# Four edits in one kernel: constants, the search, token numbers, and the order of work beside the last experts

## The chip, the cores and the metric

The kernel runs on one core of one Trainium2 chip. The metric is the time of one execution on the device in microseconds (us). The core has a matrix engine (PE, TensorE), a vector engine (DVE), a scalar engine (ACT), a general engine (POOL, GpSimd) and an engine that here only issues transfers (SP). Each runs its own instructions in order and waits on the others by semaphores. Transfers (DMAs) are issued into queues by SP, ACT or POOL and are carried out by 16 DMA engines.

## What is computed

The reference takes x of 8 x 512 tokens with 256 features. It adds to x the normalised output of an attention block with its MLP, and then the normalised output of a mixture of 8 experts. Cut to what matters here (`_layernorm` is a normalisation over the features):

```python
def experts(x, gate_w, ln_w, ln_b, fc1s, b1s, fc2s, b2s):
    xf = x.reshape(-1, d)                         # 4096 tokens, d = 256
    scores = softmax(xf @ gate_w.T)               # 4096 x 8
    vals, idx = top_k(scores.T, k)                # each expert keeps its best k = 512 tokens
    y = layernorm(xf[flat_idx].reshape(k, n, d)) * ln_w + ln_b
    h = gelu(einsum('knd,nfd->knf', y, fc1s) + b1s)          # 1024 hidden features
    out = (einsum('knf,ndf->knd', h, fc2s) + b2s) * kept_w[..., None]
    return xf.at[flat_idx].add(out.reshape(k * n, d))        # added back to the tokens' rows

x = x + _layernorm(attention_and_mlp(_layernorm(x)))
x = x + _layernorm(experts(_layernorm(x)))
```

A token may be kept by several experts or by none, so a token's row is final only when every expert that kept it has added its part.

## The kernel before

**Sizes.** P = 128 partitions, T = 4096 tokens in 8 blocks of 512 (4 tiles of 128), E = 8 experts, CAP = 512 tokens per expert in NJ = 4 tiles, NF = 8 slices of 128 hidden features, NC = 32 tiles of tokens in all.

**First stage.** It loads the weights, then for each block normalises x, computes performer attention, the MLP and the gate's logits. Constants are made first, among them the ones of the later search (lines 86 to 122): `mod_i`, `same` (a bf16 matrix that adds up the 16 partitions that hold one expert's scores), `before`, `ones_w`, `pcol`, `ccol`, `lane`, `jcol`. `pj` (line 217) is a tile that POOL sets to zero, eight small loads on ACT's queue fill, and DVE scales (line 223). Weights w1 and w2 (lines 230, 231) and the blocks of x (line 204) are loaded by SP, in this order. In this stage a planner orders the instructions of blocks that overlap.

**Search.** The 4096 x 8 scores are turned so that each partition holds 256 scores of one expert. `largest` (lines 778 to 802) finds the threshold of each expert bit by bit, 15 steps for the high bits and 15 for the low ones. A step counts on DVE the keys at or above the candidate `u` (`junk`, with the sum written to `cnt`), adds the counts over the expert's partitions on PE (`ptot`, with `same`), and gets the next candidate on DVE (`un` from `ptot` and `eb`). `low_bits` puts a few DVE instructions between.

**Token numbers.** From the threshold each kept token gets a slot from 0 to 511 (`hi` is the tile, `lo` the row in it). `mark(e)` builds on DVE a one-hot tensor `hot` (128 x 128 x 32, bf16) of `lo`, and `num` (the token's number in two parts, for the slot's tile). `number(e)` multiplies them on PE, 32 matmuls into `pi`, and DVE makes from it `idx`, the token number of every slot. `gather(e)` fetches with `idx` the token rows, by indirect DMAs that POOL issues.

**Experts.** For each expert: `hidden(e, f)` for f = 0 to 7 (two matmuls, then ACT's gelu into `hTe`), `weighted(e, j)` for j = 0 to 3 (eight matmuls, then ACT and DVE make `o`), and `add_rows(e, j)`, which adds `o` by an indirect DMA with addition to the table `accs`, for e < 4 also to the table `acc` (each scatter is preceded by a tiny memset `apart`). Beside it run `gather`, `normalised` (DVE), `keep_scores`, and `turn` (PE transposes, ACT copies) for the next expert, and the load of the expert's weights w1e, w2e after the next.

**Second half.** Here the experts' work and the last normalisation overlap. The tokens' rows in `acc` hold the sum over experts 0 to 3. For a block b of 512 tokens, `load_z` loads it on SP (buffers: 4, shared with `hot`), `S` takes mean and variance on DVE and the root on POOL (`ln_stats`, lines 129 to 138: `st`, `mv`, `rs`), `A` normalises on ACT (four activations with `nb`, a DVE instruction, lines 153 to 163), `X` adds the residual on DVE and stores the block to `out` on SP. The tokens that experts 4 to 7 keep get their final rows afterwards: `gather_sum(e)` fetches rows of `accs` into `zg` (POOL), `sum_rows` adds the expert's own `o`, `SR`, `AR`, `XR` do for them what `S`, `A`, `X` do for blocks, and `put_rows` writes them to `out` by four scatters (POOL). In the last expert this is done per tile (`finish_row`).

**Order.** From line 714 on the order is written by hand: each engine takes its instructions in the order of the program's text. `at(e, f, fn)` puts `fn` behind hidden(e, f) for f = 0 to 7, behind weighted(e, f - 8) for f = 8 to 11. Functions of one place run in the order of their registration: the loads of weights at (e, 0) and the gathers first, the list `plan` last. In `plan` a, b, c, d are experts 4, 5, 6, 7. `behind` makes a reader of a table, or the first scatter of another expert's group into it, wait for the landing of the last group of scatters.

Of the kernel before, what the change touches and what calls it, by code (L numbers as in the profile page):

```python
# [9 lines left out]
F32 = mybir.dt.float32  # L10
BF = mybir.dt.bfloat16
# [14 lines left out]
def performer_moe_kernel(  # L26
# [60 lines left out]
    mod_i = sp.tile([P, P], I32, name="mod_i")  # L87
    nc.gpsimd.iota(mod_i, pattern=[[-1, P]], base=P, channel_multiplier=1)
    nc.vector.tensor_scalar(mod_i, mod_i, E - 1, None, ALU.bitwise_and)

    same = sp.tile([P, P], BF, name="same")
    nc.vector.tensor_scalar(same, mod_i, 0.0, None, ALU.is_equal)
    before = sp.tile([P, P], BF, name="before")
    nc.gpsimd.affine_select(
        out=before, in_=same, compare_op=ALU.is_gt, fill=0.0,
        base=0, pattern=[[1, P]], channel_multiplier=-1,
    )
    ones_w = sp.tile([P, 2 * P], BF, name="ones_w")
    nc.gpsimd.memset(ones_w, 1.0)
    one_c = sp.tile([P, 1], F32, name="one_c")  # L100
    nc.gpsimd.memset(one_c, 1.0)
    pcol = sp.tile([P, 1], F32, name="pcol")
    nc.gpsimd.iota(
        pcol, pattern=[[0, 1]], base=0, channel_multiplier=1,
        allow_small_or_imprecise_dtypes=True,
    )

    ccol = sp.tile([P, NC, NJ], BF, name="ccol")
    nc.gpsimd.iota(
        ccol, pattern=[[1, 2], [2, NC // 2], [0, NJ]], base=0, channel_multiplier=0,  # L110
        allow_small_or_imprecise_dtypes=True,
    )
    lane = sp.tile([P, P, NC], BF, name="lane")
    nc.gpsimd.iota(
        lane, pattern=[[1, P], [0, NC]], base=0, channel_multiplier=0,
        allow_small_or_imprecise_dtypes=True,
    )
    jcol = sp.tile([P, NC, NJ], BF, name="jcol")
    nc.gpsimd.iota(
        jcol, pattern=[[0, NC], [1, NJ]], base=0, channel_multiplier=0,  # L120
        allow_small_or_imprecise_dtypes=True,
    )
# [70 lines left out]
    with ExitStack() as attn:  # L193
# [523 lines left out]
        for b in range(NB + 1):  # L717
            steps = [attention(b)] if b < NB else []
            steps += [mlp(b - 1)] if 0 <= b - 1 < NB else []
            steps += [gate(b - 2)] if 0 <= b - 2 < NB else []  # L720
            while steps:
                steps = [s for s in steps if next(s, s) is not s]
        with tc.manual_schedule():
            last(NB - 1)
# [53 lines left out]
    def largest(keys, tag, beside):  # L778


        u = one_c
        for i in range(15):

            scale = 2.0 ** -(14 if i == 0 else 15 - i)
            junk = rp.tile([P, W], BF, tag="junk", name=f"junk_{tag}{i}")
            cnt = small.tile([P, 1], BF, tag="cnt", name=f"cnt_{tag}{i}")
            with nc.allow_low_precision(reason="whole numbers up to 256"):
                nc.vector.scalar_tensor_tensor(
                    junk, keys, scale, u.to_broadcast([P, W]), ALU.mult, ALU.is_ge,
                    accum_out=cnt,  # L790
                )
            pt = ps_sm.tile([P, 1], F32, tag="sm", name=f"ptot_{tag}{i}")
            nc.tensor.matmul(pt, same, cnt, start=True, stop=True)
            eb = small.tile([P, 1], F32, tag="eb", name=f"eb_{tag}{i}")
            nc.vector.tensor_scalar(
                eb, u, 1.0 if i == 0 else 2.0, -0.5, ALU.mult, ALU.add
            )
            next(beside, None)
            un = small.tile([P, 1], F32, tag="un", name=f"un_{tag}{i}")
            nc.vector.scalar_tensor_tensor(un, pt, CAP - 0.5, eb, ALU.is_ge, ALU.add)  # L800
            u = un
        return u
# [3 lines left out]
    nc.vector.tensor_scalar(hs, uh, -0.5, 32768.0, ALU.add, ALU.mult)  # L806
# [5 lines left out]
    nc.vector.tensor_scalar(tl_, ul, -0.5, None, ALU.add)  # L812
# [45 lines left out]

    def mark(e, lo_e):


        num = ep.tile([P, NC, 2, NJ], BF, tag="num", name=f"num_{e}")
        nc.vector.tensor_tensor(
            num[:, :, 0, :], hi[:, e, :].unsqueeze(2).to_broadcast([P, NC, NJ]), jcol,
            ALU.is_equal,
        )
        nc.vector.tensor_tensor(num[:, :, 1, :], num[:, :, 0, :], ccol, ALU.mult)
        nc.vector.tensor_scalar(num[:, :, 0, :], num[:, :, 0, :], pcol, None, ALU.mult)
# [9 lines left out]
    def number(e):  # L878

        hot, num = hots.pop(e)  # L880
        pi = ps_sm.tile([P, 2, NJ], F32, tag="sm", name=f"pi_{e}")
        for q in range(NC):
            nc.tensor.matmul(
                pi.rearrange("p a j -> p (a j)"), hot[:, :, q],
                num[:, q, :, :].rearrange("p a j -> p (a j)"),
                start=(q == 0), stop=(q == NC - 1),
            )
        tl = small.tile([P, NJ], F32, tag="tl", name=f"tl_{e}")
        nc.vector.tensor_scalar(tl, pi[:, 1, :], float(P), None, ALU.mult)
        idx = rp.tile([P, NJ], I32, name=f"idx_{e}")  # L890
        nc.vector.tensor_tensor(idx, pi[:, 0, :], tl, ALU.add)  # L891
        idxs[e] = idx
# [146 lines left out]
    def sum_rows(e, j):  # L1039
        zj = zgs[e][:, j, 0:D]  # L1040
        nc.vector.tensor_tensor(zj, zj, rows_o[e][:, j, :], ALU.add)

    def SR(e):
        lns["r", e] = ln_stats(zgs[e], NJ, f"r{e}")
# [47 lines left out]
    for e in range(2, E):  # L1092
# [7 lines left out]
        else:  # L1100
            for j in range(NJ):
                at(e - 1, j, gather, e, range(j, j + 1))
            at(e - 1, 6, normalised, e)
            at(e - 1, 6, keep_scores, e)
# [4 lines left out]
    for e in range(L0, E):  # L1109
        for j in range(NJ):  # L1110
            at(e, (3 if e == E - 1 else 4) + j, gather_sum, e, range(j, j + 1))
            at(e, 8 + j, sum_rows, e, j)

    for b in range(3):
        at(L0, 1, load_z, b)
    a, b, c, d = range(L0, E)
    plan = [
        (a, 4, load_z, 3), (a, 6, S, 0), (a, 8, A, 0), (a, 8, S, 1), (a, 9, X, 0),
        (a, 9, load_z, 4), (a, 10, A, 1), (a, 10, S, 2), (a, 11, X, 1), (a, 11, load_z, 5),
        (a, 11, A, 2),  # L1120
        (b, 0, X, 2), (b, 0, load_z, 6), (b, 0, S, 3), (b, 2, A, 3, range(0, 2)),
        (b, 3, A, 3, range(2, 4)), (b, 4, X, 3), (b, 4, load_z, 7), (b, 4, S, 4),
        (b, 6, A, 4, range(0, 2)), (b, 7, A, 4, range(2, 4)), (b, 8, X, 4), (b, 8, S, 5),
        (b, 10, A, 5), (b, 10, SR, a), (b, 11, X, 5), (b, 11, AR, a),
        (c, 0, XR, a), (c, 0, S, 6), (c, 2, A, 6, range(0, 2)), (c, 3, A, 6, range(2, 4)),
        (c, 4, X, 6), (c, 4, S, 7), (c, 6, A, 7, range(0, 2)), (c, 7, A, 7, range(2, 4)),
        (c, 8, X, 7), (c, 8, SR, b), (c, 10, AR, b), (c, 11, XR, b),
        (d, 0, put_rows, a), (d, 1, SR, c), (d, 3, AR, c, range(0, 2)),
        (d, 4, AR, c, range(2, 4)), (d, 5, XR, c), (d, 7, put_rows, b), (d, 9, put_rows, c),
    ]  # L1130
# [3 lines left out]
    for e in range(E):  # L1134
# [12 lines left out]
        for j in range(NJ):  # L1147
# [5 lines left out]
            if e == E - 1:  # L1153
                if j > 0:
                    finish_row(e, j - 1)
                    if j == NJ - 1:
                        put_rows(e, range(j))
# [53 lines left out]
```

## Time and profile before

| | us |
|---|---|
| median of three runs | 1137.06 (1136.58 to 1138.34) |
| the profiled execution | 1131.89 |
| its span in the profile | 1130.2 |
| search, 30 steps | 802.99 to 830.3 |
| first matmul of the first `number` | 839.28 |
| expert 4, 5, 6, 7: first matmul of hidden | 981.03, 1009.45, 1050.35, 1083.86 |
| last matmul ends | 1111.58 |
| last scatter on POOL ends | 1122.30 |

The span is from the first to the last instruction of one execution that the hardware profiler recorded; the time of that execution is 1.7 us more. Times within the profile are us from the span's start. The page's rows give a line of the kernel, the engine, the operation, the tiles (written <- read) and the shapes, then total busy time, the mean in ns, and the engine's idle time ahead of the instruction with what released it. "Granted clock" is the share of PE's full speed that the throttle allowed: 0.901 over the span.

### The profile page before, as it was taken

To read this page: it belongs to the slowest core of one execution; us is meant where nothing else is said; L and a number is where in the kernel's file an instruction comes from. 1 tells how busy PE (TensorE), PEld (TensorE's weight loads), DVE (VectorE), ACT (ScalarE), POOL (GpSimd) and SP (SyncE) were. 2 spreads that over 40 slices of the span, in tenths; PEclk is the share of its full clock that TensorE was granted. 3 is DMA by queue.
4 is the path that set the end of the run, shared out by engine and by line. 5 is a ranking of instruction groups with operands and counts; after the bars stand their busy time and mean duration, and the time that the engine had idled before them with its cause. 6 is when DMAs were issued, how large, how long until landed. Compare 5 with 4: busy or idle time off the path is not lost. (4 is left out here: it accounts for less than half of the span.)

```text
span 1130.2 us, 13031 instructions
## 1 busy us (share of the span) xinstructions
PE 973.5 (86%) x4772; PEld 710.2 (63%) x4772; DVE 601.7 (53%) x1662; ACT 332.4 (29%) x618; POOL 298.5 (26%) x400
## 2 busy tenths in 40 slices
PE   2898997997999899799799799959229999997893
PEld 1685685586577568468568657848118677664562
DVE  3725637737745765773773755564762332144533
ACT  0322412423333232241332333222004222334540
POOL 5002003101200400310310120032311665555675
PEclk9958999989999999998998989979558999998997
DMA  6000000300300300120020020020531565588841
GB/s 221 1 1 1 1 1 1 113 1 1 113 1 1 112 2 1 46 68 1 1 94 1 1 94 2 1 82 13 179 111 55 107 130 119 128 274 266 235 101 56
DMA packets 61856, 77.12 MB, mean 68 GB/s; under 512 B 8032, under 2 KB 52576, under 8 KB 61664
## 3 DMA queue, kind: packets, MB, share of 16 engines
q1 hardware_dynamic: 51056, 58.87, 15.9%
q0 software_dynamic: 9920, 16.41, 7.3%
q10 hardware_dynamic: 816, 1.00, 0.3%
q8 instruction: 38, 0.62, 0.2%
q14 instruction: 26, 0.21, 0.1%
HBM read 43.09 MB, written 33.18 MB: 67 GB/s over the span
## 5 line engine op out<-in xcount | busy, mean ns | idle before, releaser
L494 PE MATMUL ph<-xaT,w_sb 128*128 128x512 f32 (+1 forms) x288 | 132.2, 587 | 0.5 <-ACT xaT L190 0.5
L1004 PE MATMUL pwe<-w2e,hTe 128*128 128x256 f32 x512 | 117.3, 387 | 6.7 <-ACT hTe L993 6.7
L989 PE MATMUL phe<-yT,w1e 128*128 128x512 f32 (+1 forms) x288 | 117.7, 567 | 4.0 <-ACT hTe L993 4.0
L520 PE MATMUL pm<-w_sb,hT 128*128 128x256 f32 x448 | 120.7, 433 | 0.0
L326 POOL TENSOR_TENSOR xn<-xn,rows_sb 128x1024 f32<-128x1024 f32 x8 | 18.7, 2341 | 364.5 <-PE pt_x L189 364.5
L1004 PEld LDWEIGHTS pwe<-w2e,hTe 128*128 128x128 f32 x512 | 98.6, 195 | 24.0 <-ACT hTe L993 8.2
L520 PEld LDWEIGHTS pm<-w_sb,hT 128*128 128x128 f32 x448 | 97.5, 222 | 18.0 <-issue 2.3
L989 PEld LDWEIGHTS phe<-yT,w1e 128*128 128x128 f32 x288 | 57.1, 200 | 58.1 <-issue 48.6
L494 PEld LDWEIGHTS ph<-xaT,w_sb 128*128 128x128 f32 x288 | 53.9, 203 | 42.6 <-issue 34.6
L385 PEld LDWEIGHTS pc<-v_aug,kp 128*128 128x128 f32 x512 | 66.9, 210 | 7.0 <-issue 3.0
L498 ACT ACTIVATE hT<-ph,cols_sb 128x512 f32<-128x512 f32 (+1 forms) x72 | 45.8, 636 | 85.9 <-PE ph L494 85.9
L409 ACT ACTIVATE qd<-qd 128x1024 f32<-128x1024 f32 x32 | 33.8, 1056 | 123.1 <-DVE qd L404 123.1
L434 PEld LDWEIGHTS po<-ctxb,qpT 128*128 128x128 f32 x512 | 64.8, 205 | 8.2 <-ACT qpT L424 4.6
L434 PE MATMUL po<-ctxb,qpT 128*128 128x34 f32 x512 | 67.2, 289 | 1.3
L385 PE MATMUL pc<-v_aug,kp 128*128 128x34 f32 x512 | 66.8, 293 | 0.9 <-DVE kp L379 0.9
L424 ACT ACTIVATE qpT<-ptq 128x512 f32<-128x512 f32 x64 | 35.2, 595 | 101.2 <-PE ptq L419 101.2
L524 DVE TENSOR_TENSOR r<-pm,r 128x256 f32<-128x256 f32 x28 | 11.9, 425 | 95.0 <-PE pm L520 95.0
L909 POOL DMA_INDIRECT accs<-o,idx x28 | 46.1, 1646 | 59.1 <-DVE o L1008 39.4
L993 ACT ACTIVATE hTe<-phe,cols_sb 128x512 f32<-128x512 f32 (+1 forms) x72 | 45.0, 636 | 54.2 <-PE phe L989 51.9
L375 ACT ACTIVATE kp<-kp,nstab 128x256 f32<-128x256 f32 x128 | 52.7, 495 | 20.7 <-DVE nstab L353 20.7
L1008 DVE SCALAR_TENSOR_TENSOR o<-b2s_sb,gg,o 128x256 f32<-128x256 f32 x32 | 15.5, 483 | 75.2 <-ACT o L1007 73.3
L895 POOL DMA_INDIRECT y<-xg,idx x32 | 35.0, 1095 | 65.4 <-DVE idx L891 38.5
(213 smaller groups left out, 1679.4 us busy)
## 6 DMA issues: line engine op xcount, KB each, us to landing
w1e<-in_f SPq DMA_DIRECT2D x8, 1024.0 KB, 8.3
w2e<-in_f SPq DMA_DIRECT2D x8, 1024.0 KB
z<-acc SPq DMA_DIRECT2D x8, 1024.0 KB
x<-in_x_in SPq DMA_DIRECT2D x8, 512.0 KB, 6.0
accs<-x SPq DMA_DIRECT2D x8, 512.0 KB, 4.0
acc<-x SPq DMA_DIRECT2D x8, 512.0 KB, 4.5
xg<-xf SPq DMA_DIRECT2D x8, 512.0 KB
accs<-xf SPq DMA_DIRECT2D x8, 512.0 KB, 4.2
```

Of the source, the lines that this page charges most:

```text
L375: nc.scalar.activation(kp[:, :, h, :], kp[:, :, h, :], AF.Exp, bias=nstab[:, h : h + 1])
L385: nc.tensor.matmul(pc[:, hp, :, :].rearrange("p a d -> p (a d)"), kp[:, t, pair, :].rearrange("p h m -> p (h m)"), v_aug[:, t, pair, :].re ...
L424: nc.scalar.activation(qpT[:, 4 * g : 4 * g + 4, :], pt, AF.Copy, bias=RATIO * EPS_K, scale=RATIO,)
L434: nc.tensor.matmul(po[:, 2 * hp : 2 * hp + 2, :].rearrange("p a d -> p (a d)"), qpT[:, hp, :], ctxb[:, hp, :, :].rearrange("p a d -> p (a ...
L494: nc.tensor.matmul(ph, w1_sb[:, c, ts(f, P)], xaTs[b][:, c, cols], start=(c == 0), stop=(c == KD - 1),)
L498: nc.scalar.activation(hTs[b][:, f, cols], ph, AF.Relu, bias=cols_sb[:, C_B1 + f : C_B1 + f + 1])
L520: nc.tensor.matmul(pw, hT[:, f, ts(t, P)], w2_sb[:, f, :], start=(f == 0), stop=(f == NF - 1),)
L895: this = nc.gpsimd.indirect_dma_start(out=dst, out_offset=None, in_=table[:, :], in_offset=bass.IndirectOffsetOnAxis(ap=idx[:, j : j + 1], ...
L909: this = nc.gpsimd.indirect_dma_start(out=table[:, :], out_offset=bass.IndirectOffsetOnAxis(ap=idxs[e][:, j : j + 1], axis=0), in_=src, in ...
L989: nc.tensor.matmul(ph, w1e[:, c, ts(f, P)], yT[:, c, cols], start=(c == 0), stop=(c == KD - 1))
L993: nc.scalar.activation(hTs[e][:, f, cols], ph, AF.Gelu_apprx_tanh, bias=cols_sb[:, col : col + 1])
L1004: nc.tensor.matmul(pw, hT[:, f, ts(j, P)], w2e[:, f, :], start=(f == 0), stop=(f == NF - 1))
```

## The change

The four parts:

- **Constants.** The block of lines 87 to 122 moves behind the steps of block 0 in the first stage. New constants come with it: `same_far` (`same` times 2^18), `bias_c`, `top`, `bit_steps` (15 pairs, written by 30 small memsets).
- **Search.** The count is a `tensor_scalar` against `u` as a per-partition operand instead of a `scalar_tensor_tensor` against `u` broadcast. A bias matmul opens the sum on PE, the count's matmul with `same_far` ends it, so that `ptot` is a large number with the sign of the answer; `un` clamps it between the two next candidates `lh`.
- **Token numbers.** In `number` the operands change sides: a slice of `num` with 32 columns is held in PE and `hot` streams, and four matmuls write to four groups of 32 partitions of `pq`. DVE copies `pq` to `quarters`, and an fp32 matmul with `pick` adds up the four groups into `pi`. `num` lies in two fixed tiles, set to zero once.
- **Order beside experts 4 to 7.** `plan` is rewritten, `normalised` and `keep_scores` go from (e-1, 6) to (e-1, 7) for the late experts, `sum_rows` of all four tiles becomes part of `SR`, and the last expert's `put_rows` goes in pieces of 2, 1 and 1 tiles instead of 3 and 1.

```diff
@@ constants: the moved block stands behind the steps of block 0 @@
+            if b > 0:
+                continue
+            mod_i = sp.tile([P, P], I32, name="mod_i")
...
+            FAR = 2.0 ** 18
+            same_far = sp.tile([P, P], BF, name="same_far")
+            nc.vector.tensor_scalar(same_far, same, FAR, None, ALU.mult)
+            bias_c = sp.tile([P, 1], BF, name="bias_c")
+            nc.gpsimd.memset(bias_c, -float(CAP // (P // E)))
+            nc.gpsimd.memset(bias_c[0:E, :], 0.5 - float(CAP // (P // E)))
+            top = sp.tile([P, 1], F32, name="top")
+            nc.gpsimd.memset(top, 2.0 ** 14 - 0.5)
+            bit_steps = sp.tile([P, 15, 2], F32, name="bit_steps")
+            for i in range(15):
+                down, up = (-(2.0 ** (13 - i)), 2.0 ** (13 - i)) if i < 14 else (-1.0, 0.0)
+                nc.gpsimd.memset(bit_steps[:, i, 0:1], down)
+                nc.gpsimd.memset(bit_steps[:, i, 1:2], up)
...
@@ def largest(keys, tag, beside): @@
+            nc.tensor.matmul(pt, same_far, bias_c, start=True, stop=False)
             with nc.allow_low_precision(reason="whole numbers up to 256"):
-                nc.vector.scalar_tensor_tensor(
-                    junk, keys, scale, u.to_broadcast([P, W]), ALU.mult, ALU.is_ge,
-                    accum_out=cnt,
+                nc.vector.tensor_scalar(
+                    junk, keys, u, 0.0, ALU.is_ge, ALU.add, accum_out=cnt
                 )
-            pt = ps_sm.tile([P, 1], F32, tag="sm", name=f"ptot_{tag}{i}")
-            nc.tensor.matmul(pt, same, cnt, start=True, stop=True)
-            eb = small.tile([P, 1], F32, tag="eb", name=f"eb_{tag}{i}")
-            nc.vector.tensor_scalar(
-                eb, u, 1.0 if i == 0 else 2.0, -0.5, ALU.mult, ALU.add
-            )
+            nc.tensor.matmul(pt, same_far, cnt, start=False, stop=True)
+            lh = small.tile([P, 2], F32, tag="lh", name=f"lh_{tag}{i}")
+            nc.vector.tensor_tensor(lh, u.to_broadcast([P, 2]), bit_steps[:, i, :], ALU.add)
             next(beside, None)
             un = small.tile([P, 1], F32, tag="un", name=f"un_{tag}{i}")
-            nc.vector.scalar_tensor_tensor(un, pt, CAP - 0.5, eb, ALU.is_ge, ALU.add)
+            nc.vector.scalar_tensor_tensor(
+                un, pt, lh[:, 0:1], lh[:, 1:2], ALU.max, ALU.min
+            )
@@ ahead of mark @@
+    CT = P // 4
+    nums = []
+    for i in range(2):
+        nm = rp.tile([P, NC, CT], BF, name=f"num{i}")
+        nc.gpsimd.memset(nm, 0.0)
+        nums.append(nm)
+    pick_i = rp.tile([P, CT], I32, name="pick_i")
+    nc.gpsimd.iota(pick_i, pattern=[[-1, CT]], base=P, channel_multiplier=1)
+    nc.vector.tensor_scalar(pick_i, pick_i, CT - 1, None, ALU.bitwise_and)
+    pick = rp.tile([P, 2 * NJ], F32, name="pick")
+    nc.vector.tensor_scalar(pick, pick_i[:, 0 : 2 * NJ], 0.0, None, ALU.is_equal)
@@ def number(e): @@
         hot, num = hots.pop(e)
+        pq = ps_sm.tile([P, P], F32, tag="sm", name=f"pq_{e}")
+        for r in range(NC // 4):
+            for c in range(4):
+                q = 4 * r + c
+                nc.tensor.matmul(
+                    pq[c * CT : (c + 1) * CT, :], num[:, q, :], hot[:, :, q],
+                    start=(r == 0), stop=(r == NC // 4 - 1),
+                )
+        quarters = small.tile([P, P], F32, tag="quarters", name=f"quarters_{e}", bufs=2)
+        nc.vector.tensor_copy(quarters, pq)
         pi = ps_sm.tile([P, 2, NJ], F32, tag="sm", name=f"pi_{e}")
-        for q in range(NC):
-            nc.tensor.matmul(
-                pi.rearrange("p a j -> p (a j)"), hot[:, :, q],
-                num[:, q, :, :].rearrange("p a j -> p (a j)"),
-                start=(q == 0), stop=(q == NC - 1),
-            )
+        nc.tensor.matmul(
+            pi.rearrange("p a j -> p (a j)"), quarters, pick, start=True, stop=True
+        )
@@ the second half @@
-    def sum_rows(e, j):
-        zj = zgs[e][:, j, 0:D]
-        nc.vector.tensor_tensor(zj, zj, rows_o[e][:, j, :], ALU.add)
+    def sum_rows(e, js=range(NJ)):
+        zg = zgs[e][:, js[0] : js[-1] + 1, 0:D]
+        nc.vector.tensor_tensor(zg, zg, rows_o[e][:, js[0] : js[-1] + 1, :], ALU.add)
 
     def SR(e):
+        sum_rows(e)
         lns["r", e] = ln_stats(zgs[e], NJ, f"r{e}")
...
-            at(e - 1, 6, normalised, e)
-            at(e - 1, 6, keep_scores, e)
+            at(e - 1, 7, normalised, e)
+            at(e - 1, 7, keep_scores, e)
...
-            at(e, 8 + j, sum_rows, e, j)
-
-    for b in range(3):
-        at(L0, 1, load_z, b)
     a, b, c, d = range(L0, E)
     plan = [
-        (a, 4, load_z, 3), (a, 6, S, 0), (a, 8, A, 0), (a, 8, S, 1), (a, 9, X, 0),
-        (a, 9, load_z, 4), (a, 10, A, 1), (a, 10, S, 2), (a, 11, X, 1), (a, 11, load_z, 5),
-        (a, 11, A, 2),
-        (b, 0, X, 2), (b, 0, load_z, 6), (b, 0, S, 3), (b, 2, A, 3, range(0, 2)),
-        (b, 3, A, 3, range(2, 4)), (b, 4, X, 3), (b, 4, load_z, 7), (b, 4, S, 4),
-        (b, 6, A, 4, range(0, 2)), (b, 7, A, 4, range(2, 4)), (b, 8, X, 4), (b, 8, S, 5),
-        (b, 10, A, 5), (b, 10, SR, a), (b, 11, X, 5), (b, 11, AR, a),
-        (c, 0, XR, a), (c, 0, S, 6), (c, 2, A, 6, range(0, 2)), (c, 3, A, 6, range(2, 4)),
-        (c, 4, X, 6), (c, 4, S, 7), (c, 6, A, 7, range(0, 2)), (c, 7, A, 7, range(2, 4)),
-        (c, 8, X, 7), (c, 8, SR, b), (c, 10, AR, b), (c, 11, XR, b),
-        (d, 0, put_rows, a), (d, 1, SR, c), (d, 3, AR, c, range(0, 2)),
-        (d, 4, AR, c, range(2, 4)), (d, 5, XR, c), (d, 7, put_rows, b), (d, 9, put_rows, c),
+        (a, 1, load_z, 0), (a, 3, load_z, 1), (a, 5, load_z, 2), (a, 6, S, 0), (a, 8, S, 1),
+        (a, 8, load_z, 3), (a, 10, A, 0), (a, 10, S, 2), (a, 11, X, 0), (a, 11, A, 1),
+        (b, 0, S, 3), (b, 0, load_z, 4), (b, 1, X, 1), (b, 2, A, 2, range(0, 2)),
+        (b, 2, load_z, 5), (b, 3, A, 2, range(2, 4)), (b, 4, S, 4), (b, 4, X, 2),
+        (b, 5, A, 3, range(0, 2)), (b, 5, load_z, 6), (b, 6, A, 3, range(2, 4)),
+        (b, 6, S, 5), (b, 7, X, 3), (b, 8, A, 4), (b, 8, load_z, 7), (b, 8, SR, a),
+        (b, 9, X, 4), (b, 10, A, 5), (b, 10, S, 6), (b, 11, X, 5), (b, 11, AR, a),
+        (c, 0, S, 7), (c, 1, XR, a), (c, 2, A, 6, range(0, 2)), (c, 3, A, 6, range(2, 4)),
+        (c, 3, SR, b), (c, 4, X, 6), (c, 5, A, 7, range(0, 2)), (c, 6, A, 7, range(2, 4)),
+        (c, 7, X, 7), (c, 10, AR, b), (c, 11, XR, b),
+        (d, 0, SR, c), (d, 0, put_rows, a), (d, 2, AR, c, range(0, 2)),
+        (d, 3, AR, c, range(2, 4)), (d, 4, XR, c), (d, 7, put_rows, b), (d, 8, put_rows, c),
     ]
...
@@ the loop over experts, in the last expert's weighted @@
                 if j > 0:
                     finish_row(e, j - 1)
-                    if j == NJ - 1:
-                        put_rows(e, range(j))
+                if j == 2:
+                    put_rows(e, range(0, 2))
+                if j == 3:
+                    put_rows(e, range(2, 3))
+                sum_rows(e, range(j, j + 1))
                 lns["r", e, j] = ln_stats(zgs[e][:, j : j + 1, :], 1, f"r{e}_{j}")
```

## The prediction, made before the changed kernel ran

> **What bounds it now.** I read the page first: its totals, the 40 slices, then the span in windows by stage, what PE waited for, and the order of time on each engine around those waits.
>
> ```profile
> span 1130.2 us, 13031 instructions
> PE 973.5 (86%) x4772; PEld 710.2 (63%) x4772; DVE 601.7 (53%) x1662; ACT 332.4 (29%) x618; POOL 298.5 (26%) x400
> PE   2898997997999899799799799959229999997893
> PEclk9958999989999999998998989979558999998997
> DMA  6000000300300300120020020020531565588841
> ```
> A slice is 28.3 us. PE is at 9 or more in most of them: until about 800 us (attention and its MLP) and again from 840 (the experts) matmuls set the time. The two 2s (slices 29 and 30) are the search, a ladder of tiny steps between DVE and PE; the last digit is the tail without matmuls. In the second half of the experts the DMA row rises to 8.
>
> ```profile
> 985.00:1018.00 33.00, 31.48 (x112) 20.10 (x110) 13.96 (x42) 11.86 (x22) 20.00 (x23) 1.00 0.89 273
> 1018.00:1050.00 32.00, 25.88 (x87) 17.84 (x88) 15.54 (x46) 14.80 (x28) 19.30 (x21) 0.84 0.84 262
> 1050.00:1084.00 34.00, 30.94 (x108) 20.50 (x107) 16.69 (x49) 16.60 (x32) 21.76 (x26) 0.95 0.70 192
> 1084.00:1112.00 28.00, 27.57 (x97) 17.91 (x95) 10.13 (x25) 9.64 (x18) 21.41 (x33) 1.00 0.35 97
> ```
> Columns: stretch, length, busy PE, PEld, DVE, ACT, POOL, granted clock, DMA share, GB/s. Expert 4 is within the first row, 5 within the first and second, 6 in the third, 7 in the fourth: only 5 and 6 lose PE time, and with it clock (0.84).
>
> ```profile
> PE pwe L1004 <- ACT hTe L993: 6.7, 2, 3.7
> PE phe L989 <- ACT hTe L993: 4.0, 1, 4.0
> ```
> These are all of PE's waits after 980 us: three, 10.7 us, each for hTe, ACT's output. The first shows what held ACT up:
>
> ```profile
> 1014.73 1.67 POOL L136 TENSOR_SCALAR rs_z<-mv_z 128x4 f32<-128x4 f32 x1
> 1016.49 1.04 POOL L137 TENSOR_TENSOR rs_z<-rs_z,mhalf 128x4 f32<-128x4 f32 x1
> ```
> ```profile
> 1017.76 2.07 ACT L161 ACTIVATE z<-z,nb_z,rs_z 128x256 f32<-128x256 f32 x4 [3.56 <-DVE nb_z L156]
> 1019.74 1.81 ACT L993 ACTIVATE hTe<-phe,cols_sb 128x512 f32<-128x512 f32 x3
> ```
> ```profile
> 1020.46 2.08 PE L989 MATMUL phe<-yT,w1e 128*128 128x512 f32 x2 [3.98 <-ACT hTe L993]
> ```
> POOL's root for block 2 (S, 2) ended at 1017.5, ACT sat in A(2) ahead of hTe, PE idled 3.98. Undisturbed, an expert takes 28.4 us (e4: 981.03 to 1009.45; it is 8 × 1.717 hidden, 4 × 3.46 weighted, 1.04 turn). e5 took 40.9 (1009.45 to 1050.35), e6 33.5 (to 1083.86): 17.6 us over, 10.7 of it waits, the rest a slow clock after them (16 matmuls 10.05 us instead of 7.03 after the first).
>
> **The late plan.** Loads. z0 to z3 wait for the scatters into acc and for buffers, not for PE, and SP runs ahead: all four went at 990.6 to 993.1, and in the new places they go at the same time. That "spread" costs and brings nothing. SP's queue matters later:
>
> ```profile
> 1006.55 0.38 SPq L1035 DMA_DIRECT2D out<-z  x1
> 1009.48 0.36 SPq L1016 DMA_DIRECT2D z<-acc  x1
> ...
> 1019.75 0.56 SPq L738 DMA_DIRECT2D w1e<-in_f  x1
> 1020.36 0.46 SPq L740 DMA_DIRECT2D w2e<-in_f  x1
> ```
> z4 needs z0's buffer, so it follows the landing of out0 (2.9 us). Now X(0) is issued at (a,11), some 5.5 us later (1012), and w1e, w2e of expert 6, registered at (b,0) ahead of load_z 4, go before z4: 2 MB at 262 to 273 GB/s are 7.8 us, z4's 1 MB 3.9, so z4 lands near 1012.5 + 7.8 + 3.9 = 1024.2.
>
> Roots. S(0) and S(1) move ahead, A(0) behind the last two outputs of expert 4, A(2) to (b,2): the 3.98 wait at 1016 should go, with about 3 us of clock. But DVE's new order is S(4), X(2), nb of block 3: S(4) waits for z4, and behind it stands what A(3) and so hTe need. z4 1024.2 + S(4) 2.3 (4 × 0.401, 4 × 0.182) + X(2) 1.2 + nb 0.2 + A(3) 2.1 + hTe 0.6 = 1030.6. PE ends e5's hidden at 1009.45 + 13.7 = 1023.2 and has six of eight matmuls of weighted(5,0), 2.6 us, before it stops: a wait of 4.8, and 1.5 of clock, half of what the first cost. So e5 = 28.4 + 6.3 = 34.7, and e6 starts at 1044.2 (1050.35). In e6 the loads have lead (DMA falls to 0.70); a third of its 5.1 over stays possible, I take 1.0: e7 starts at 1073.6, 10.3 earlier.
>
> Tail. From e7's start POOL is the chain:
>
> ```profile
> 1087.31 1.03 POOL out L909
> ```
> That is put_rows(a)'s first scatter, at 3.45 after e7's start. Now SR(c) stands ahead of it at (d,0), with all of sum_rows: 1.22 + 4 × 0.406 + 4 × 0.182 = 3.6, then the root on POOL, so put a starts about 4.1 later, and the gathers of e7, put b, put c and the last group follow in series (scatters at 1.31 us pitch). Last scatter 42.8 after e7's start instead of 38.4: +4.4. The last group's rows go as 2, 1, 1 instead of 3, 1: at most one scatter's 1.3 earlier or an added wait on the landing (2.4) later; I take 0. Sum of the late part: −10.3 + 4.4 = −5.9. Bounds: −11 (no new wait in e5, less tail) and +4 (a new wait of 15).
>
> **The search.** 30 steps at 0.883 us.
>
> ```profile
> L788 DVE SCALAR_TENSOR_TENSOR junk_l<-kc,un_l 128x256 bf16<-128x256 f32 x14 | 5.9, 424 | 0.5
> L800 DVE SCALAR_TENSOR_TENSOR un_l<-ptot_l,eb_l 128x1 f32<-128x1 f32 x15 | 2.4, 159 | 2.9 <-PE ptot_l L793 2.9
> L809 DVE SCALAR_TENSOR_TENSOR kc<-khs,hs,kl 128x256 f32<-128x256 f32 x1 | 0.5, 485 | 0.0
> ```
> The count becomes a TENSOR_SCALAR with a per-partition operand and an accumulator. No such row exists. `above` (L816), the same form without accumulator, took 353; the immediate form of `khs` 281; the two-tensor form takes 424, with a per-partition operand (kc) 485. So the count lies between 281 and 485; I take 424, the row of the present accumulating count. un gains per-partition operands: 0 to 61 ns, I take 30. lh takes eb's place (148) beside the matmul, and the bias matmul (163) runs under the count; uncovered, these would be 0.15 each a step. Sum 30 × 0.03 = +0.9; bounds 30 × −0.143 = −4.3 and 30 × 0.122 = +3.7. [...]
>
> **Numbers by column tiles.** The first stands on the path to the first gather:
>
> ```profile
> 839.28 2.27 PE L883 MATMUL pi<-num,hot 128*128 128x8 bf16 x32 [4.36 <-DVE hot L872]
> ```
> 32 loads of 128 columns and matmuls of 8 become 32 loads of 32 columns and matmuls of 128, four side by side; then a DVE copy of 128x128 from PSUM (about 0.29) and an fp32 matmul with 8 columns (0.2), with hand-overs 0.75. What the 32 save is unknown: 0 to 1.4, so −0.65 to +0.75 each; the middle, 0, for all eight, and ±5 as bounds. In the seven others PE stands still during the copy, and hidden's matmuls wait behind it. [...]
> pick_i, pick: two small DVE instructions ahead of the first mark, +0.3. The two memsets of num lie on POOL, which is idle in the search.
>
> **Start.** The first BN starts at x0's landing (16.34). Constants leave POOL's first 7 us; none was on the path. But pj's eight small loads on ACT's queue come forward (their tile's memset at 7.39 is now first), and the DMA semaphores are taken in turn: in the built program w2's load now waits for w1's landing, about 12, where it was issued at 3.58, and x0 stands behind it on SP (4.35 before). w1, w2 and x0 come at 380 GB/s; the queues run dry about 2 us, partly filled by small loads: +1.2, bounds −0.2 and +3. It carries on, as all attention follows x0. pj's scale (2.55, at 22.40) moves ahead, which brings nothing: block 1's xn waits for POOL's root at 24.63.
>
> **Sum:** −5.9 + 0.9 + 0 + 0.3 + 1.2 = −3.5. On the profiled execution (1131.89; span 1130.2 and 1.7 around it) this gives 1128.4. The median of the runs is 1137.06, 5.2 above it; so 1133.6.
>
> **Rivals.** (1) The late waits vanish wholly: for it, DVE, ACT and POOL are under 65% busy in the first three windows; against it, the DMA share of 0.84 and the two weight loads ahead of z4. It takes 6.3 and 1.0 more off: 1126.3.
> (2) Slower: z4's late landing. Its price is one us of PE for each us after 1019.4 (1024.2 less the 4.8), and z5 follows out1 behind it. The late part is worth nothing once the e5 wait and clock reach 12.2, z4 at about 1029; at the 66 to 75 GB/s of the poorest slices beside the gathers it can be there. With z4 at 1034, a 15 us wait: late +4, with the rest +6.4: 1143.5.
> (3) POOL's tail takes PE's gain, since put_rows and gathers are chained by their landings: late part −2, with the rest about 0: 1137.5. For it: in the last window POOL, at 21.4 of 28, is busy second only to PE, and the end hangs on POOL; against it: part of that was waiting for e7's rows.
>
> **Chances.** About 0.2% (2.3 us) is what runs of this kernel can tell from no change. Forecast 0.45 (0.32 faster, 0.10 same, 0.03 slower, by the search's and number's bounds; own range 1129 to 1139), rival 1 0.20 (faster), rival 2 0.23 (slower), rival 3 0.12 (0.05 same, 0.07 slower). Faster 0.52, same 0.15, slower 0.33. The range reaches to 1125 for rival 1 and to 1143.5 for rival 2.
>
> **What would show it.** Search steps: the row of junk, 424 by me, 485 or 353 by the others; the ladder's length (27.3). number: PE's 32 matmuls and the gap before pi. First BN at 17.5. No PE wait near 1016 to 1020 after e5's start, one of 4 to 7 in weighted(5,0) with S(4) waiting for z4; e7's start 10 earlier; put a 7.5 after it. I am wrong if e5 keeps its first wait, if number loads stretch PE by more than 1 us each, or if z4 lands past 1029.

## The result and the profile after

| | before | changed | |
|---|---|---|---|
| median, 11 runs each | 1136.58 us (1127.39 to 1141.18) | 1144.99 us (1143.01 to 1150.13) | ratio 1.0089, 95% interval 1.0064 to 1.0115: slower |
| profiled execution, span | 1130.2 | 1142.8 | +12.6 |

The forecast was 1133.6 us, faster, with 1125 to 1143.5 as its range. The change is slower, and its median lies above the range. The page's head and slices of the changed kernel:

```profile
span 1142.8 us, 13146 instructions
## 1 busy us (share of the span) xinstructions
PE 974.1 (85%) x4818; PEld 704.0 (62%) x4818; DVE 602.8 (53%) x1664; ACT 333.0 (29%) x618; POOL 301.4 (26%) x435
...
PE   2898997997999899799799799868228999997991
...
PEclk9857999999999999998998999969559999998996
DMA  6000000300300200120020020020711554579941
```
PE is as busy as before (974.1 against 973.5 us) and the span 12.6 longer, so on balance nearly all of it is time in which PE did nothing. The granted clock reads 9, 8, 5, 7 in the first four slices, where before it read 9, 9, 5, 8. That says nothing of the change: `p4_late` below, whose first stage is before's, reads 9, 8, 5, 7 too. To see where the time came from, the two traces are cut at the same instructions; a table of differences says more here than any total:

| stretch | before | changed | difference | forecast |
|---|---|---|---|---|
| start to the first count of the search | 802.99 | 806.45 | +3.46 | +1.2 |
| to the first matmul of the first `number` | 36.29 | 39.77 | +3.48 | +1.2 (search, `pick`) |
| to expert 4's first matmul | 141.75 | 149.80 | +8.05 | 0 |
| expert 4 to expert 7 | 102.83 | 95.59 | −7.24 | −10.3 |
| expert 7 to the end of the last scatter | 39.53 | 44.35 | +4.82 | +4.4 |
| to the end of the span | 6.81 | 6.84 | +0.03 | |

(The last scatter of before starts at 1122.30 and ends at 1123.39; the table of times before the change gives the first of the two as its end.) The first row's +3.46 can't all be put down to the change, since this stage is not equally long in all executions; how much is told below.

Each row has its lines in the trace. First the start, before (SP's queue, and DVE's first batch-norm statistics of x, "the first BN"):

```profile
3.58 0.72 SPq L231 DMA_DIRECT2D w_sb<-in_w  x1
4.35 12.35 SPq L204 DMA_DIRECT2D x<-in_x_in  x4
```
```profile
16.34 0.75 DVE L134 BATCH_NORM_STATS2 st_a<-x 128x6 f32<-128x256 f32 x2 [14.09 <-DMA x<-in_x_in]
```
And in the changed kernel:

```profile
11.70 0.37 SPq L195 DMA_DIRECT2D w_sb<-in_w  x1
12.12 3.86 SPq L168 DMA_DIRECT2D x<-in_x_in  x4
```
```profile
19.09 0.75 DVE L98 BATCH_NORM_STATS2 st_a<-x 128x6 f32<-128x256 f32 x2 [5.38 <-DMA x<-in_x_in]
```
w2's load is issued at 11.70 instead of 3.58, x behind it at 12.12 instead of 4.35, and the first BN, which waits for x in both, starts at 19.09 instead of 16.34. The rows of the search, by forms:

```profile
L805 DVE TENSOR_SCALAR_CACHE_REDUCE junk_l<-kc,un_l 128x256 bf16<-128x256 f32 x14 | 6.7, 480 | 0.5
...
L813 DVE SCALAR_TENSOR_TENSOR un_l<-ptot_l,lh_l 128x1 f32<-128x1 f32 x15 | 3.3, 218 | 2.8 <-PE ptot_l L803 2.6 <-PE ptot_l L808 0.2
```
The accumulating count has a name of its own in the trace and takes 480 ns (424 before); `un` 218 (159). One number in the expert loop, PE in order of time:

```profile
871.20 2.02 PE L915 MATMUL pq<-hot,num 128*32 128x128 bf16 x32
873.62 0.39 PE L922 MATMUL pi<-pick,quarters 128*128 128x8 f32 x2 [0.39 <-DVE quarters L920]
873.86 2.84 PE L1026 MATMUL phe<-yT,w1e 128*128 128x256 f32 x12
```
The same number before:

```profile
863.78 2.01 PE L883 MATMUL pi<-num,hot 128*128 128x8 bf16 x32
865.65 2.84 PE L989 MATMUL phe<-yT,w1e 128*128 128x256 f32 x12
```
The 32 matmuls take 2.02 us, as the 32 of before (1.96 to 2.08 in the loop). Then PE waits 0.39 for the copy and spends 0.24 on the fp32 matmul until its next one. So hidden goes on 2.66 us after the first of the 32, where it went on after 1.87: 0.79 later, and nothing has been saved.

The late part, in windows from expert 4's start: expert 4, 5, 6, 7 (the columns as before):

```profile
996.00:1024.40 28.40, 28.40 (x105) 19.05 (x104) 9.07 (x34) 10.91 (x18) 16.35 (x18) 1.00 0.84 260
1024.40:1063.20 38.80, 31.70 (x106) 20.67 (x106) 20.43 (x60) 18.10 (x34) 24.86 (x27) 0.87 0.88 267
1063.20:1091.60 28.40, 28.40 (x105) 19.06 (x104) 13.46 (x34) 16.41 (x30) 20.97 (x26) 1.00 0.82 232
1091.60:1119.40 27.80, 27.72 (x97) 18.05 (x95) 8.29 (x18) 9.16 (x17) 20.78 (x31) 1.00 0.37 91
```
Expert 6 now runs without a gap (28.4), expert 5 takes 38.8, with 7.1 us of idle PE. In the changed kernel the chain behind that gap, on DVE, ACT and PE:

```profile
1042.53 0.43 DVE L98 BATCH_NORM_STATS2 st_z<-z 128x6 f32<-128x256 f32 x1 [10.77 <-DMA z<-acc]
```
```profile
1045.97 1.09 ACT L125 ACTIVATE z<-z,nb_z,rs_z 128x256 f32<-128x256 f32 x2 [10.34 <-DVE nb_z L120]
```
```profile
1047.69 1.22 PE L1041 MATMUL pwe<-w2e,hTe 128*128 128x256 f32 x2 [6.76 <-ACT hTe L1030]
```
S(4) waits on DVE for z4 until 1042.53, A(3) on ACT for the `nb` behind it, PE for the hTe behind A(3). z4 was issued at 1030.31, behind the weights of expert 6, and took 12.2 us. SP's queue:

```profile
1027.31 0.45 SPq L753 DMA_DIRECT2D w1e<-in_f  x1
1027.87 0.94 SPq L755 DMA_DIRECT2D w2e<-in_f  x1
1030.31 0.37 SPq L1053 DMA_DIRECT2D z<-acc  x1
```
And the tail. The first scatter of put_rows(a) starts 7.5 us after expert 7's first matmul (1091.61), where it started after 3.45:

```profile
1099.15 1.11 POOL L946 DMA_INDIRECT out<-zg,idx  x1 [0.17 <-issue]
```

### The profile page after: what moved, and what is told of

It is laid out like the page before. It is cut to its first block, busy times and chain, and to the rows that moved or that the text cites. A ratio compares the mean times of both kernels' runs of the same rounds, so it can differ in the third digit from the quotient of the medians.

```text
span 1142.8 us, 13146 instructions
## 1 busy us (share of the span) xinstructions
PE 974.1 (85%) x4818; PEld 704.0 (62%) x4818; DVE 602.8 (53%) x1664; ACT 333.0 (29%) x618; POOL 301.4 (26%) x435
## 4 chain that ended last, share of the span: by engine, by line
PE 76%; DVE 10%; POOL 5%; issue 2%; ACT 2%; DMA 2%; another core or an unknown queue 0%; POOLq 0%; ACTq 0%; DVEq 0%; SPq 0%
PE pm L484 10%; PE ph L458 10%; PE pwe L1041 8%; PE phe L1026 7%; PE po L398 6%; PE pc L349 6%; PE pxk L265 3%; PE pxq L265 3%; PE pw L425 3%; PE pk L229 3%; PE pq L229 3%; PE ptq L383 2%; PE pv L322 2%; DVE r L110 1%; PE pl L544 1%
## 5 line engine op out<-in xcount | busy, mean ns | idle before, releaser
L1026 PE MATMUL phe<-yT,w1e 128*128 128x512 f32 (+1 forms) x288 | 114.0, 553 | 0.0
```

The lines of the kernel that those rows point to most:

```text
L1026: nc.tensor.matmul(ph, w1e[:, c, ts(f, P)], yT[:, c, cols], start=(c == 0), stop=(c == KD - 1))
```

## The experiments

Twelve kernels ran, each beside runs of before on the same chip; a pair of numbers in brackets is the 95% interval of the ratio to before. A warning for reading their profiles: the first stage is not equally long in all executions of what is there the same program. The first count of the search came between 797.5 and 809.1 us in the profiles of kernels whose first stage is before's. So each part is read from its own stretch, and the whole from the ratio of many runs.

### One part at a time

**Constants alone** (`p1_start`): the block of constants moved as in the change, without the new ones.

> Only the constants' move of the change. If w2's load waits for w1's landing and the first block of x stands behind it, as the changed kernel's trace has it (w2 issued at 11.70, first BN at 19.09 instead of 16.34), this alone has its first BN at 19.1 and its first count of the search 2.7 to 3.5 us later than before's 802.99, and is 2.7 to 3.5 us slower. Rival: the 30 memsets and new constants on POOL made the delay; then the first BN stays at 16.3 and the time is the same.

Measured: 1.0033 (1.0008 to 1.0058), about 3.7 us; first BN 18.62 (15.2 to 16.6 in the profiles of all kernels but this and the changed one). The rival falls: there are no new constants in this kernel, and it is late all the same.

**Search alone** (`p2_search`): `largest` of the change, its constants beside the old ones.

> Only the search of the change, its constants made where the old ones were. If the accumulating count takes 479 ns and un 216 whatever stands around them, the 30 steps take 30 x 0.11 = 3.4 us more and the kernel is 3.0 to 3.8 us slower. Rival: these durations came with the changed kernel's slower clock or its POOL work; then the rows are at 424 and 158 and the time is the same within 1 us.

Measured: 1.0029 (1.0007 to 1.0052), about 3.3 us; the count at 479 ns, the stretch from the first count to the first `number` 39.56 (36.29). The durations belong to the instructions.

**Numbers alone** (`p3_numbers`): `mark`, `number`, `num` and `pick` of the change.

> Only the token numbers by four column tiles. If PE's 32 matmuls keep their 64 ns pitch and each number adds the wait for the copy and the fp32 matmul (0.85 us), seven in the expert loop and the first one add 6.5 to 8.5 us at the start of expert 4, and the kernel is as much slower, less what the late waits give back. Rival: in the changed kernel the expert loop was late for another reason (the gathers); then expert 4 starts less than 3 us later.

Measured: 1.0067 (1.0045 to 1.0089), about 7.6 us. From the first `number` to expert 4 it takes 147.66 (141.75): +5.9. The stretch before it is 1.29 longer, where the forecast had 0.3 (`pick`). DVE and POOL of this kernel, early in the search:

```profile
810.49 1.75 DVE L773 CAST kl<-lb_i 128x256 f32<-128x256 int32 x1
812.16 0.14 DVE L800 SCALAR_TENSOR_TENSOR un_h<-ptot_h,eb_h 128x1 f32<-128x1 f32 x1
```
```profile
810.25 1.84 POOL L863 MEMSET num<- 128x1024 bf16 x2
```
The cast took 0.28 in before. Here it ends as POOL's memsets of `num` do (812.24 and 812.09), and `un` of the ladder, at 812.16, stands behind it. In `n_outer` below, which has the same memsets, the cast takes 1.74. In the changed kernel it took 0.51, from 807.99 to 808.49, and ended 0.15 after the first of the two memsets (808.35); the next instruction of that kind, `khs`, took 0.40 instead of 0.28 and ended 0.15 after the second.

**Late order alone** (`p4_late`): `plan`, `sum_rows`, the places of `normalised` and `put_rows` of the change.

> Only the order beside experts 4 to 7. From the changed kernel's profile: expert 4's start unchanged at 981, expert 5 loses about 10 us in one wait in weighted(5,0), expert 6 nothing, so expert 7 starts 7.2 us earlier; the tail after it 4.9 longer: 1.5 to 3.5 us faster. By the forecast's own terms (one wait of 4.8 and 1.5 of clock) it would be 5.9 faster. Rival: the late part lived on the others' delay; then it is not faster.

Measured: 1.0002 (0.9980 to 1.0025). The profile gives what was expected in both directions: expert 4 to 7 in 96.62 (102.83), the tail 44.30 (39.53), so −1.4, which the interval (−2.3 to +2.8 us) holds and can't tell from nothing. The forecast's −5.9 is not in it. The four parts add up to 1.0131, each ± 0.0025, so ± 0.005 together; the whole was 1.0089 ± 0.0025. That agrees, so nothing here says that the parts work on each other.

### Why the constants' move costs

`start_pj`: the same move, but with pj's memset, loads and scale behind the other tiles:

```diff
-        nc.gpsimd.memset(pj, 0.0)
         nc.sync.dma_start(wk_sb, wk.rearrange("(c p) o -> p c o", p=P))
...
             ctxs.append(cb)
+        nc.gpsimd.memset(pj, 0.0)
+        for h in range(HC):
+            nc.scalar.dma_start(pj[h * DH : (h + 1) * DH, h, :], projT)
+        nc.vector.tensor_scalar(pj, pj, NORM, None, ALU.mult)
```


> Only the constants' move, but with pj's memset, eight loads and scale behind hsel, v_aug and ctxb in the program, so that w2's load waits for the landing of cols and the first x for that of wk, as before. If the delay came from w2 waiting for w1's landing, w2 is issued near 3.6 again, the first BN is at 15 to 16.5 (18.6 with the move alone), and the time is before's or up to 1 us faster. Rival: POOL's and DVE's new order is what delays; then the first BN stays past 18.

Measured: 1.0002 (0.9973 to 1.0031); first BN 16.56. SP's queue of this kernel:

```profile
2.82 0.47 SPq L190 DMA_DIRECT2D w_sb<-in_w  x1
3.66 0.38 SPq L191 DMA_DIRECT2D w_sb<-in_w  x1
4.09 13.39 SPq L168 DMA_DIRECT2D x<-in_x_in  x4
```
w2 and x are issued at 3.66 and 4.09 again, with the constants still moved. The delay was not the constants but the eight small loads that their move let go ahead. What w2's load waited for, before and in the changed kernel:

```profile
SPq L231 <- DMA cols_sb<-in_cols: 0.3, 1, 0.3
```
```profile
SPq L195 <- DMA w_sb<-in_w: 8.4, 1, 8.4
```
In the two traces SP's and ACT's first loads share eight semaphores (100 to 107 in the trace), which they take in turn, and a load waits for the landing of the one that had its semaphore before it. Before, w2 took 100, that of the short load `cols` (40 KB), and waited 0.3 us; with seven of pj's loads ahead of it in the turn, it takes 106, that of w1, and waits 8.4 us for 1 MB.

### Why four column tiles save nothing

`n_outer`: as `p3_numbers`, with the two loops changed over, so that eight matmuls in a row hit the same column tile:

```diff
-        for r in range(NC // 4):
-            for c in range(4):
+        for c in range(4):
+            for r in range(NC // 4):
```


> Only the token numbers by column tiles, with the loops changed over: eight matmuls in a row go to the same column tile before the next. If four tiles side by side are what lets 128 columns be streamed at a pitch of 64 ns, the pitch now rises to 90 ns or more and the 32 matmuls take 2.9 us or more instead of 2.0. Rival: the pitch is set by the issue of the load and the matmul, whatever they hold; then they stay at 2.0 and the tiles bring nothing.

Measured: 1.0388 (1.0330 to 1.0446). PE of this kernel:

```profile
897.62 4.46 PE L898 MATMUL pq<-hot,num 128*32 128x128 bf16 x32
902.46 0.59 PE L905 MATMUL pi<-pick,quarters 128*128 128x8 f32 x2 [0.38 <-DVE quarters L903]
902.91 6.53 PE L1024 MATMUL pwe<-w2e,hTe 128*128 128x256 f32 x16
```
4.46 us for 32 is 139 ns each, against 63 with the tiles side by side. So the tiles do run beside each other and more than halve the pitch. But 63 to 64 ns is also the pitch of before, whose matmuls had 8 columns to stream instead of 128: the tiles pay for the columns that the swap of operands brought in, and no more. What remains is the copy and the second matmul. Why both forms come out at the same pitch no run here shows. The last line shows a second cost of this order: 16 matmuls that take 3.70 us in `p3_numbers` take 6.53 here, with a granted clock of 0.50 in the 3.1 us after the number (1.00 there). That accounts for most of what this kernel lost beyond 27 us (the 7.6 of `p3_numbers` and eight times 2.46), 44 in all: such slow matmuls followed six of the seven numbers in the loop, and cost 2.4 to 2.8 us each time.

### What of the search costs

`s_oldcount`: the search alone, with the count back as a `scalar_tensor_tensor`:

```diff
-                nc.vector.tensor_scalar(
-                    junk, keys, u, 0.0, ALU.is_ge, ALU.add, accum_out=cnt
+                nc.vector.scalar_tensor_tensor(
+                    junk, keys, 1.0, u.to_broadcast([P, W]), ALU.mult, ALU.is_ge,
+                    accum_out=cnt,
                 )
```


> Only the search of the change, but with the count as scalar_tensor_tensor against u broadcast. If count and un each put what they take more on the path, the count is back at 424 and the steps' pitch is 0.883 + 0.058 = 0.94 us: the search takes 1.7 us more than before's, half of the 3.4. Rival: the bias matmul or lh is on the path too; then the pitch stays above 0.96.

Measured: 1.0011 (0.9984 to 1.0038); count 425, `un` 218, and the stretch to the first `number` 37.91, 1.62 longer than before's and 1.65 shorter than `p2_search`. Half is the count and half `un`; the bias matmul and `lh` are hidden.

### Where the late order loses

Three edits of the late order alone, and two of them together:

```diff
@@ l_tail: before's places in the last expert @@
-        (d, 0, SR, c), (d, 0, put_rows, a), (d, 2, AR, c, range(0, 2)),
-        (d, 3, AR, c, range(2, 4)), (d, 4, XR, c), (d, 7, put_rows, b), (d, 8, put_rows, c),
+        (d, 0, put_rows, a), (d, 1, SR, c), (d, 3, AR, c, range(0, 2)),
+        (d, 4, AR, c, range(2, 4)), (d, 5, XR, c), (d, 7, put_rows, b), (d, 9, put_rows, c),
@@ l_sdve: S(4) behind A(3) @@
-        (b, 6, S, 5),
+        (b, 6, S, 4), (b, 6, S, 5),
@@ l_w: expert 6's weights behind load_z 5 @@
-            at(e, 0, lambda e=e: ws.__setitem__(e + 1, load_expert(e + 1)))
+            at(e, 3 if e == 5 else 0, lambda e=e: ws.__setitem__(e + 1, load_expert(e + 1)))
```
(In `l_sdve` S(4) leaves (b, 4).)

> The late order alone, with before's places of put_rows a, b, c and SR c, AR c, XR c in the last expert; the last expert's scatters stay at 2, 1, 1. If put a waiting behind the root of SR c makes the tail long, the stretch from expert 7's start to the last scatter falls from 44.3 to about 40 and the kernel is 1.4 + 4.3 = 5.7 us faster than before. Rival: the tail is long because gathers and scatters follow one another's landings, or through the 2, 1, 1; then it stays at 44 and the time near 1.4 faster.

Measured: 0.9981 (0.9952 to 1.0011); the tail 41.49, 2.8 shorter than with the late order (44.30) where 4.3 was expected. The order around put a is most of the tail's loss; the other 2.0 stays open, and 1.3 of it lies within what before's own late order shows (39.53 to 40.81 in the profiles of kernels that have it).

> The late order alone, with S(4) on DVE moved from (b, 4) behind A(3) at (b, 6). If S(4), which waits for z4, ahead of nb of block 3 is what holds ACT and so hTe, PE's wait in weighted(5,0) of 7.6 goes, expert 5 takes 28.4 to 32 instead of 39.8, and expert 7 starts 6 to 10 us earlier than with the late order. Rival: the wait moves on to A(4) and o of expert 5 on ACT behind it; then expert 5 gains less than 4.

Measured: 0.9989 (0.9960 to 1.0018); expert 4 to 7 in 96.39, no gain. The rival is right that the wait moves on, but not about where. DVE and PE of this kernel:

```profile
1035.25 0.43 DVE L134 BATCH_NORM_STATS2 st_z<-z 128x6 f32<-128x256 f32 x1 [5.84 <-DMA z<-acc]
...
1037.39 1.13 DVE L957 TENSOR_SCALAR y<-y 128x256 f32<-128x256 f32 x4
```
```profile
1037.83 2.07 PE L974 MATMUL pt_y<-ident,y 128*128 128x128 f32 x8 [8.66 <-issue]
```
PE idles 8.66 us at the turn of expert 6's tokens. It starts as soon as the first of their tiles is normalised on DVE (`y`), and that now stands behind S(4) and S(5), which wait for z4 and z5. A(4) on ACT stood 14.04 us for its `nb`, but PE didn't wait for it.

> The late order alone, with the two loads of expert 6's weights behind load_z 5 on SP, at (b, 3). If their 2 MB ahead of z4 make it late, z4 lands 5 to 8 us earlier (18 us after expert 5's start until now), the wait in weighted(5,0) falls from 7.6 to under 2, and expert 7 starts 7 to 10 us earlier than with the late order. Rivals: z4 comes late because of the other transfers (gathers, scatters, out), then the wait stays over 5; or the weights come late for expert 6, then PE waits for w1e at its start.

Measured: 0.9964 (0.9931 to 0.9997). z4 is there 12.4 us after expert 5's start instead of 18.9, and expert 5 takes 31.0 instead of 39.8. But expert 6 takes 36.3 instead of 28.4, and from 4 to 7 it is 95.79: the wait has moved on by one expert. PE of this kernel:

```profile
1021.49 0.70 PE L1004 MATMUL pwe<-w2e,hTe 128*128 128x256 f32 x2 [1.08 <-ACT hTe L993]
...
1034.97 7.03 PE L989 MATMUL phe<-yT,w1e 128*128 128x512 f32 x16
1046.12 9.80 PE L989 MATMUL phe<-yT,w1e 128*128 128x512 f32 x16 [4.12 <-ACT hTe L993]
```
PE did not wait for expert 6's weights, which the second rival feared, but for hTe again.

> Both together and before's place of the last scatters (3 and 1): expert 7 starts 14 to 16 us earlier than before's 102.8 after expert 4, the tail is 40 to 44, and the kernel is 8 to 14 us faster than before (ratio 0.988 to 0.993). If the tail hangs on the DMAs' landings, a large part of it is given back: 4 to 8 faster.

Measured: 0.9952 (0.9924 to 0.9980), 95.45 from expert 4 to 7 and a tail of 43.4: faster than before, by some 5 us, the lower case of the expectation. Its trace shows the wait in expert 6: S(6) on DVE stands 5.14 us for z6, and the `nb` for AR(a), which ACT has to do before the next hTe, is behind it. So `l_best` moves that, on top of `l_wtail`:

```diff
-        (b, 10, A, 5), (b, 10, S, 6), (b, 11, X, 5), (b, 11, AR, a),
-        (c, 0, S, 7), (c, 1, XR, a), (c, 2, A, 6, range(0, 2)), (c, 3, A, 6, range(2, 4)),
-        (c, 3, SR, b), (c, 4, X, 6), (c, 5, A, 7, range(0, 2)), (c, 6, A, 7, range(2, 4)),
-        (c, 7, X, 7),
+        (b, 10, A, 5), (b, 11, X, 5), (b, 11, AR, a),
+        (c, 0, XR, a), (c, 2, S, 6), (c, 4, A, 6, range(0, 2)), (c, 5, A, 6, range(2, 4)),
+        (c, 5, SR, b), (c, 6, X, 6), (c, 6, S, 7), (c, 8, A, 7, range(0, 2)), (c, 9, A, 7, range(2, 4)),
+        (c, 9, X, 7),
```


> The late order with expert 6's weights behind load_z 5, before's tail, and S(6), S(7) with their A and X later in expert 6, so that AR a and hTe don't stand behind z6. If z6's wait (4.46 to 5.14 on DVE) ahead of AR a's nb is what moved PE's stall into expert 6, expert 6 takes 28.4 to 31 instead of 36, experts 4 to 7 take 88 to 91 instead of 95.4, and with the tail at 43 the kernel is 8 to 12 us faster than before. Rival: the gain goes into a longer tail on POOL, since scatters follow gathers there; then the tail is 47 or more and the time stays near 0.995.

Measured: 0.9914 (0.9881 to 0.9947), median 1122.90 against 1131.76: faster than both kernels, by about 9 us against before. Experts 4 to 7 as one window of this kernel:

```profile
977.50:1066.70 89.20, 86.50 (x313) 56.80 (x313) 43.10 (x128) 43.85 (x81) 60.10 (x67) 1.00 0.88 268
```
89.2 us instead of 102.9, where three undisturbed experts are 85.3, and the granted clock is 1.00 (0.93 in the same stretch of before). DVE still waits for z there, 24.1 us in all, but what PE needs next no longer stands behind it: from expert 4 on, PE's waits are five, 4.8 us together, 2.1 of them at most at once. The tail is 44.0 against 39.5 in before's profile; what is left of the loss is there, and no run here shows why it is that long.

## Why the prediction was wrong

The forecast's sum was −3.5 us, the two profiles give +12.6, a miss of 16.1. Half of it is the numbers, the other half the three other parts. Step by step:

- **Numbers, 0 forecast, +8 measured.** This is the largest miss, and the step that failed: a term put at nothing. The forecast set the unknown saving of the 32 matmuls between 0 and 1.4 us, without a row for either end, and took the middle. The row it quoted held matmuls of 8 columns (64 ns each in the loop); with 128 columns four tiles side by side take 63. The saving is 0, and the copy and the second matmul stay: 0.95 on the path of the first number (3.26 from its first matmul to `tl` instead of 2.31) and 0.77 for each of the seven others (PE's next matmul comes 2.67 after the first of the 32 in `p3_numbers`, 1.90 before, on average), which is the forecast's upper bound of +0.75 and not its middle. Together that is 6.3, of which 5.9 show in `p3_numbers` from the first number on; the changed kernel has 2 more, 1.6 of it one long wait for a copy (2.03 instead of 0.39) whose cause is not shown. The bounds of ±5 were too narrow even by the forecast's own figures: eight times +0.75 is 6.
- **Search, +0.9 forecast, +3.3 measured (`p2_search`).** The mechanism and the bound (+3.7) were right, the value was not: the count was put at 424, the row of an instruction with two tensors and an immediate, instead of 485, the row with a per-partition operand; it took 479. `un` with its per-partition operands took 59 ns more (218 against 159); the forecast took 30. The form with an accumulator did not run like `above`, the same form without one (353).
- **Constants, +1.2 forecast, +2.75 at the first BN.** The mechanism (w2 behind w1's landing, x behind w2) is shown by `start_pj`. It was mis-sized: x landed at 19.1, not 17.5. Over many runs `p1_start` puts this part at 3.7 us, with an interval from 0.9 to 6.6.
- **Late order, −5.9 forecast, −2.4 measured.** Right: the old waits go, the loads' spread does nothing (z0 to z3 were issued together again, at 1004.90), one new wait comes in weighted(5,0), through S(4), z4 and the weights ahead of it, expert 6 is whole, put a starts 7.5 after expert 7's start. The tail is longer by +4.82, with +4.4 forecast; that the two agree so well is in part luck, since undoing the order around put a (`l_tail`) gave back 2.8 and not 4.1. Mis-sized: the new wait and the clock behind it. z4 was put 14.75 us after expert 5's start and came 18.1 after it. Its issue came as forecast (5.9 after the start; X(0) and out0's landing gave 5.5), but its transfer took 12.2 from there, where the forecast left it 9.3. The way from z4 to PE was 5.2 instead of 6.4, since hTe stands behind half of A(3) and not all of it. So PE's waits were 7.1 instead of 4.8, the slow clock after them cost 3.2 instead of 1.5, and expert 5 lost 10.3 and not 6.3.
- **The rivals.** Rival 2 named the right place, z4, and it was late, but not past the point from which it would have decided (1029 in the forecast's terms, 19.6 after expert 5's start). Rival 3 (POOL's tail takes PE's gain) holds of this part in size: `p4_late` alone is 1.0002, 6.2 gained and 4.8 given back. None of the rivals had three small costs at their upper bounds together, and the range, built from the late part, left that out: with the late part as forecast, the other parts' own upper bounds (6, 3.7, 0.3 and 3) give 1144.2, which is above the range and near the measured 1144.99.

## What to carry to other kernels

Before a rewrite that uses more of an engine at once, look at the pitch of what is there. If the old form is already at the pitch of the new one (64 and 63 ns here), every added hand-over is a loss (0.77 us each here), and it counts once for each time the in-order engine stands for it. A wait that is taken out of a chain of loads comes back where the next load is needed, so move the work that waits for it away from what the busiest engine's inputs stand behind, for every load of the chain, not for the first; here the first such move only brought the wait into the next expert (95.8 us for three experts instead of 96.6), and moving the later ones too brought 89.2. And price small instructions by a row with the same kinds of operands (the count took 479 ns; such a row had 485, the one that was taken 424).

## What was not expected of the hardware

- While two memsets ran on POOL (1.84 us together in `p3_numbers`), a cast on DVE from SBUF to SBUF took 1.75 us instead of 0.28 and ended 0.15 us after them; in `n_outer`, with the same memsets, it took 1.74. The ladder's next step, which uses POOL for nothing, stood behind it. What held the cast is not shown, nor why in the changed kernel it came in after the first memset (0.51 us). The accumulating counts that ran there during the memsets took their usual 478 ns.
- In `n_outer`, after the number at 897.62 (4.46 us, one column tile at a time), the granted clock was 0.50 for 3.1 us and 0.59 for the next 3.2, with PE busy all the time; after the same matmuls over four tiles in `p3_numbers` it was 1.00. Six of the seven numbers in the loop were followed by matmuls slowed so, the one at 921.38 was not; what sets it off stays open.
- The same first stage took from 797.5 to 809.1 us in different executions, more than the whole effect of the change; parts of it could be told only by their own stretch or over many runs.
